# A transformer block with self- and cross-attention: where the context norm is turned, which output goes first, and when weights and x are asked for

## The chip, the cores and the metric

The kernel runs on one core of a Trainium2 chip. The metric is the device time in microseconds (us) of one execution. A core has a matrix engine (PE, or TensorE), a vector engine (DVE), a scalar engine (ACT), a general engine (POOL, or GpSimd) and a queue engine (SP) which issues nearly all DMA transfers here. Each engine works through its own list of instructions in the order in which the program wrote them; an instruction that waits holds up everything behind it on the same engine.

## The reference

All is float32, with B = 2 batches, S = 1024 positions, width D = 256, a context of T = 154 positions of width 192, 16 heads of 64, and a feed-forward width of 1024.

```python
h = layernorm(x, ln1_g, ln1_b)
x = attention(h, h, sa_wq, sa_wk, sa_wv, sa_wo, sa_bo) + x
h = layernorm(x, ln2_g, ln2_b)
x = attention(h, ctx, ca_wq, ca_wk, ca_wv, ca_wo, ca_bo) + x
h = layernorm(x, ln3_g, ln3_b)
p = h @ ff_w1 + ff_b1
a, gate = p[..., :1024], p[..., 1024:]
out = (a * gelu(gate)) @ ff_w2 + ff_b2 + x
# attention: q, k, v by heads; softmax(q k^T / 8) v; heads joined; @ wo + bo
```

## The kernel before

The work is written out by hand in program order; no scheduler moves it. It has three loops, and the pieces of other stages are laid between their steps.

**Self-attention** goes over 16 units (two batches times eight pairs of heads), each in 8 slots, so there are 128 attention slots, numbered p from 0. A slot treats 128 queries of a pair of heads, in two groups of 64. It begins with `self_first`: 32 score matmuls (L465) into two PSUM tiles `s`, and two maxima on DVE (`st`, L627). Then `then()` writes four exponentials on ACT (L476, with their sums). Since a row of scores is split over two groups of partitions, the maxima and sums have to be swapped between them: `exchange` (L486), four small DMAs on SP, issued when the slot's exponentials are done. One slot later `join` corrects for the two maxima (POOL `dd`, ACT `ee`, POOL `zz` and `den`), DVE takes a reciprocal (`rd`, L573) and POOL scales the exponentials (L577). Two slots later DVE transposes them into `pT` (L591), and `self_values` multiplies by v (`po`, L512). The reciprocal is written on DVE ahead of the next slot's maxima, and `ee` on ACT behind the next slot's exponentials, so an exchange that lands late holds up both engines.

The slots of the first half of a unit (n = 0, 1, and in unit 0 up to 3) and those at n = 4, 5 have no `self_values`; there `run_work` puts in the next unit's projections (`pq_sa`, `pk_sa`, L348, `pv_sa`, L379), a step of a norm from the list `side`, and output projections (`py`, L443) from the list `outs`. v's projection of units 1 to 3 is made in two halves, each in a slot of its own. When v is complete, two DMAs of 256 KB in all exchange its halves between partitions (L392, L393).

After `then()` a slot takes one entry of the list `later` (in every slot below 32, afterwards in three slots of eight), and then `load_ahead` asks for the weights of the unit after next: q at slot n = 2 of a unit, k at 3, v at 7 (q and k three slots later in unit 0). All of these are issued on SP behind the slot's exchange. `load_ahead_parts` (L146) makes the loads of the second batch's x (eight tiles of 128 KB) and of sa_wo (eight chunks of 128 KB), which `later` holds from the start, after unit 1's k and q weights and an empty entry.

**Cross-attention** goes over the same 16 units in three slots each, n = 0, 1, 2: 48 cross slots, numbered c. A slot makes scores of up to three tiles against 154 context positions (`sc`, L746), maxima (`neg`), up to six exponentials on ACT (L762), and a slot later their scaling on POOL (L773); DVE transposes them (L789), SP regroups them (L806), and `cross_weigh` at n = 1 multiplies by v (`cross_values`, `poc`, L825). What lies beside:

- n = 0: q of the next unit (`pq_ca`, copied to SBUF by ACT at the next slot, L363);
- n = 1: k of the next unit (`pk_ca`, L690), a step of `side`, the context's v in every other unit (`pv_ca`, L706, copied by three ACT instructions, L715 and L716), up to two outputs, then `poc`;
- n = 2: a step of `side`, and up to two outputs.

A step of a norm (`norm_pieces`, `norm_beside`) takes the statistics of two tiles on DVE, the deviation on POOL, normalises two tiles (`xn`, on POOL for the second batch's context norm at L253, on ACT for the feed-forward norm at L256), and turns two earlier ones: four transposes on PE into one PSUM bank (`ph`, L266), which ACT copies into `hT` with gain and shift (L281). The copies of a step (`store`) wait in the list `stores`, which is flushed after the next slot's scores, or at n = 1 ahead of `poc`, behind the slot's exponentials. A step that turns needs a PSUM bank: `run_work(n, n_side, bank, n_sum)` gives it `bank`, or spends one of its n `mm` banks; without either it stops at such a step and takes no step behind it.

PSUM has three rings of two: `s` (two banks each), `mm` and `po` (one bank each; `mm_tile` and `sum_tile`). A ring gives its buffers in turn, so a matmul that opens a buffer waits until the one before has been copied out. From the third unit on, `pk_ca` uses `po`'s ring, as do the first half of `poc` (two banks), the steps that turn, and the outputs counted by n_sum. The second half of `poc` uses `mm`.

**The feed-forward part** runs in 64 slots (`pa`, L907; `pf`, L930). At the seam between self- and cross-attention, the first cross slot begins with `cross_keys` of unit 1, which needs that unit's ca_wk; the tile for k weights has one buffer, that for q weights two.

Of the kernel before, what the change touches and what calls it, by code (L numbers as in the profile page):

```python
# [18 lines left out]
def tile_transformer_block(ctx: ExitStack, tc: tile.TileContext, a: dict, out: bass.AP):  # L19
    nc = tc.nc  # L20
# [8 lines left out]
    NPAIR = DA // (2 * DH)  # L29
# [13 lines left out]
    QG = 2 * KB  # L43
# [101 lines left out]

    def load_ahead_parts():  # L146

        wo["sa"] = const.tile([P, NPAIR, D], F32, tag="wo", name="sa_wo")

        def tile_of_x(t):  # L150
            nc.sync.dma_start(
                out=xt[B - 1, t // GT][:, t % GT, :], in_=x[B - 1, t * P:(t + 1) * P, :])

        def chunk(i):
            nc.sync.dma_start(out=wo["sa"][:, i, :], in_=w["sa_wo"][i * P:(i + 1) * P, :])

        return ([lambda t=t: tile_of_x(t) for t in tile_order("sa")],
                [lambda i=i: chunk(i) for i in range(NPAIR)])

    for what in "qkv":  # L160
        load_weights("sa", 0, what)
# [128 lines left out]
    def tile_order(kind):  # L290

        if kind == "ff":
            return list(range(NT))
        return [t for i in range(NT // 2) for t in (i, NT // 2 + i)]
# [75 lines left out]
            else:  # L370
                nc.scalar.copy(dk, own)  # L371

    def project_self_values(v, pv, wt, h, i0, n):

        for i in range(i0, i0 + n):
            for c in range(NH):
                for r in range(2):
                    own = slice(r * HR, (r + 1) * HR)
                    nc.tensor.matmul(  # L379
                        pv[r][:, i * P:(i + 1) * P], lhsT=h[own, c, i * P:(i + 1) * P],  # L380
                        rhs=wt[own, c, :], start=(c == 0), stop=(c == NH - 1),
                        tile_position=(r * HR, 0),
                    )

        def store():
            tiles = [slice(r * GT + i0, r * GT + i0 + n) for r in range(2)]
            for r in range(2):
                nc.scalar.copy(
                    v[:, tiles[r], 0, :],
                    pv[r][:, i0 * P:(i0 + n) * P].rearrange("p (t d) -> p t d", d=P))  # L390
            if i0 + n == GT:
                nc.sync.dma_start(out=v[:QG, :, 1, :], in_=v[QG:, :, 0, :])  # L392
                nc.sync.dma_start(out=v[QG:, :, 1, :], in_=v[:QG, :, 0, :])  # L393

        return store

# [29 lines left out]

        return [costing(2, q), costing(2, k)] + value_pieces(b, pr, parts)

    def value_pieces(b, pr, parts):
        n = GT // parts  # L430
        return [
            costing(2, lambda i=i: project_self_values(
                qk["sa", b, pr][2], two_banks(f"pv_sa{b}_{pr}_{i}"), wsl["sa", pr, "v"],
                hT["sa", b], i * n, n))
            for i in range(parts)
        ]

# [223 lines left out]
    def load_ahead(p):  # L661

        ui, n = divmod(p, 2 * SH)
        for what in "qkv":
            at = {"q": 2, "k": 3, "v": 2 * SH - 1}[what] + 3 * (ui == 0 and what != "v")
            if n != at:
                continue
            if ui + 2 < NU:
                load_weights("sa", units[ui + 2][1], what)
            elif ui + 2 == NU or what == "q":  # L670
                load_weights("ca", units[ui + 2 - NU][1], what)
        if p >= SA - 2:
            load_weights("ca", units[1][1] if p == SA - 2 else units[2][1], "kq"[p - SA + 2])


    CG = [(t, min(TG, NT - t)) for t in range(0, NT, TG)]
# [275 lines left out]
    with tc.manual_schedule():  # L952
# [46 lines left out]
        take("k", 0)  # L999
        part("k", 3)  # L1000
        take("k", 2)
        tiles, chunks = load_ahead_parts()
        later.append(lambda: load_weights("sa", units[1][1], "k"))
        later.append(lambda: load_weights("sa", units[1][1], "q"))
        later.extend([lambda: None] + tiles + chunks)
        side.append((True, (), turn_rows))
        side.extend((True, (), lambda b=b: turn_context(b)) for b in range(B))
        work.append(costing(2, lambda: self_queries(*units[0], P, 2 * P)))
        work.extend(value_pieces(*units[0], 2))

        for p in range(SA):
            if p % (2 * SH) == 0:
                self_beside(p // (2 * SH))
            if p == SA - SH:
                work.extend(held)
                held.clear()
            then = self_first(p)
            flush(stores)
            late = then()
            if p >= LAG:  # L1020
                turn_groups(p - LAG)
            flush(adds)
            if late:
                late()
            if later and (p < 2 * SH * HP or p % (2 * SH) in (2, 4, 6)):
                later.pop(0)()
            load_ahead(p)
            h, hg = divmod(p, SH)
            if h == 0 or hg < LAG:

                run_work(2 if p < SA - SH else 1, h % 2 or h == 0, sum_tile)
                if p == LAG:
                    load_weights("sa", units[1][1], "v")
            else:
                run(lambda: self_values(h - 1, hg - LAG))

        for c in range(CA):
            if c == 0:
                pTc["ring"] = pt_.tile(
                    [P, 2 * NK, QH // 2], F32, tag="pT", name="pT_ca"  # L1040
                ).rearrange("p a b -> p (a b)")[:, :3 * 2 * NB * NT * KB].rearrange(
                    "p (u n j q) -> p u n j q", u=3, n=NB, j=2)
            if c == SH + 1:
                out_pieces("sa", B - 1, 1, tile_order("ca"))
                outs.append(lambda: load_out("ca"))
            if c == SH + 1:

                w1, w2, parts = hold_gated()
                add_biases("ca", 0)
                others = later[:] + [lambda: None] * (len(parts) - len(later))  # L1050
                later[:] = [fn for pair in zip(parts, others) for fn in pair] + others[len(parts):]
            ui, n = divmod(c, len(CG))
            nxt = units[ui + 1] if ui + 1 < NU else None
            if n == 0:
                cross_beside(ui)
            elif n == 1 and 1 <= ui < NU - 2:
                load_weights("ca", units[ui + 2][1], "q")
            elif n == 2:
                for i, what in ((2, "k"), (1, "v")):
                    if 1 < ui + i < NU:  # L1060
                        load_weights("ca", units[ui + i][1], what)
            if c == 0:
                run(lambda: cross_keys(*nxt))
            flush(adds)
            then = cross_first(c)
            flush(stores)
            if c == 1:
                turn_groups(SA - 2)
            if n == 1 and ui > 1 and nxt:
                run(lambda: cross_keys(*nxt, sum_tile))  # L1070
                flush(stores)
            flush(drain)
            flush(lates)
            lates.append(then())
            if c == 0:
                drain.append(scale_groups(*joins.pop(0)))
            if c == 2:
                turn_groups(SA - 1)
            cross_drain(c)
            if c == 1:  # L1080
                run(lambda: cross_queries(*nxt))
            elif c == 2:
                run(lambda: cross_queries(*units[2], bank=sum_tile))
            elif c == 3:
                run(lambda: self_values(2 * NU - 1, 0))
            elif c == 4:
                run(lambda: self_values(2 * NU - 1, 1))
                run(lambda: cross_keys(*nxt, sum_tile))
            elif n == 0 and ui:
                if nxt:  # L1090
                    run(lambda: cross_queries(*nxt))
                run_work(0, 1)
            elif n == 1:

                run_work(0, 1, sum_tile)
                if ui % 2 == 0:
                    run(lambda: context_values(*units[ui]))
                run_work(0, 0, n_sum=1)
                run_work(1, 0)
                flush(adds)  # L1100
                flush(stores)
                cross_weigh(c)
            elif n == 2:
                run_work(0, 1, sum_tile)
                if len(outs) > 2:
                    run_work(2, 0)
            cross_regroup(c)
            for _ in range(min(2, len(later))):
                later.pop(0)()
# [58 lines left out]
```

## Time and profile before

| what | us |
|---|---|
| median of 3 runs (1149.77 to 1154.18) | 1152.45 |
| profiled execution | 1153.73 |
| its span, first to last instruction | 1151.9 |

The stretches of the profiled span, by where the first score matmul of a unit or stage starts, and how much of each PE is busy:

| stretch | length | PE busy | DVE busy | ACT busy |
|---|---|---|---|---|
| start, to the first scores | 17.55 | 13.17 | 9.05 | 7.59 |
| unit 0 | 44.64 | 40.90 | 33.05 | 28.49 |
| unit 1 | 46.69 | 43.82 | 39.49 | 27.71 |
| unit 2 | 43.28 | 40.91 | 39.22 | 28.39 |
| unit 3 | 43.83 | 41.40 | 39.75 | 30.01 |
| units 4 to 15 | 524.73 | 522.21 | 474.72 | 347.24 |
| cross-attention, from the seam | 231.64 | 218.93 | 147.56 | 136.16 |
| feed-forward | 199.54 | 195.02 | 53.42 | 41.03 |

A line of a list of waits names the engine, its tile and line, who ended the wait, and then the total in us, the number of times and the longest. A line of a timeline has its start, its length, the engine, line and operation, the tiles as out<-in, shapes and a count; in brackets stands the idle time ahead of it and who ended it. A line of windows has the stretch, its length, and then for PE, weight loads, DVE, ACT and POOL the busy us with the number of instructions, then the granted clock of PE, the share of the DMA engines that is busy, and GB/s.

### The profile page before, as it was taken

The page shows a single profiled execution, that of the slowest core. Times are in us where ns is not written, and L with a number is a line of the kernel's source. Part 1 is how long each engine was busy: PE and PEld are TensorE (multiplying, and loading weights), DVE is VectorE, ACT ScalarE, POOL GpSimd, SP SyncE. Part 2 cuts the span into 40 slices and gives each one's busy share as a digit, 9 for nine tenths or more (in the row PEclk, how much of TensorE's full clock was granted, in tenths as well). Part 3 has the DMA queues.
Part 4 walks back from the last instruction along what each step waited for, and adds up shares of the span by engine and source line. Part 5 has one row for each costly group of instructions (what it writes and reads, how often), then busy time and mean ns, then how long its engine had stood idle before and what let it go on. Part 6 is the DMA issues. An engine that isn't in the chain of part 4 may idle for free.

```text
span 1151.9 us, 36754 instructions
## 1 busy us (share of the span) xinstructions
PE 1116.4 (97%) x14372; PEld 687.6 (60%) x14372; DVE 836.3 (73%) x1183; ACT 646.6 (56%) x2082; POOL 675.9 (59%) x1568
## 2 busy tenths in 40 slices
PE   8899999999999999999999999998999989999998
PEld 6444444545545545545445554675667667888887
DVE  4888998898888998999898889665666764232222
ACT  5665666666765665666666666557555571041111
POOL 2666777778777877777777777656454443020000
PEclk9999999999999999999999999999999999999999
DMA  3222112101111111111111110257554533000000
GB/s 88 62 68 67 35 31 47 41 13 40 39 23 40 33 28 45 31 30 40 31 30 40 25 28 15 65 141 188 137 119 115 119 78 74 10 10 10 19 10 19
DMA packets 104910, 59.94 MB, mean 52 GB/s; under 512 B 32090, under 2 KB 95522, under 8 KB 104738
## 3 DMA queue, kind: packets, MB, share of 16 engines
q1 hardware_dynamic: 103506, 56.93, 20.8%
q8 instruction: 114, 1.87, 0.7%
q10 hardware_dynamic: 1232, 0.66, 0.2%
q14 instruction: 58, 0.48, 0.1%
HBM read 27.91 MB, written 2.10 MB: 26 GB/s over the span
## 4 chain that ended last, share of the span: by engine, by line
PE 80%; ACT 7%; DVE 4%; DMA 3%; issue 2%; POOL 2%; SPq 2%; DVEq 0%; ACTq 0%; POOLq 0%
PE po L512 17%; PE s L465 17%; PE pa L907 10%; PE py_sa L443 5%; PE pf L930 5%; PE py_ca L443 4%; PE pk_sa L348 4%; PE pq_sa L348 4%; PE poc L825 4%; PE pv_sa L379 4%; ACT p L476 3%; PE pq_ca L348 3%; ACT p L762 2%; PE sc L746 2%; DMA st<-st 2%
## 5 line engine op out<-in xcount | busy, mean ns | idle before, releaser
L476 ACT ACTIVATE p<-s,st 128x512 f32<-128x512 f32 x512 | 345.2, 686 | 205.1 <-DVE st L627 201.5
L577 POOL TENSOR_SCALAR p<-p,rd,ee 128x512 f32<-128x512 f32 x512 | 387.5, 774 | 45.1 <-DVE rd L573 44.0
L627 DVE TENSOR_REDUCE st<-s 128x2 f32<-128x1024 f32 x256 | 301.2, 1218 | 36.0 <-PE s L465 24.9
L591 DVE STREAM_TRANSPOSE pT<-p 128x1024 f32<-128x1024 f32 x256 | 302.2, 1218 | 0.4 <-POOL p L577 0.3
L465 PE MATMUL s<-k_sa,q_sa 64*32 64x512 f32 x4096 | 253.2, 596 | 12.7 <-ACT p L476 11.9
L512 PE MATMUL po<-pT,v_sa 64*64 64x256 f32 x4096 | 236.7, 380 | 0.0
L512 PEld LDWEIGHTS po<-pT,v_sa 64*64 64x64 f32 x4096 | 150.7, 133 | 109.9 <-issue 31.0
L773 POOL TENSOR_SCALAR p<-p,rden 128x154 f32<-128x154 f32 x256 | 97.4, 404 | 101.2 <-DVE rden L770 100.7
L762 ACT ACTIVATE p<-sc,neg 128x154 f32<-128x154 f32 x256 | 96.9, 418 | 91.3 <-DVE rden L770 84.9
L465 PEld LDWEIGHTS s<-k_sa,q_sa 64*32 64x32 f32 x4096 | 65.4, 106 | 136.5 <-issue 66.0
L907 PE MATMUL pa<-hT_ln,wf 128*128 128x256 f32 x512 | 120.7, 379 | 0.0
L916 DVE SCALAR_TENSOR_TENSOR u<-pa,cols,gate 128x256 f32<-128x256 f32 x64 | 30.9, 483 | 123.2 <-ACT gate L913 123.2
L913 ACT ACTIVATE gate<-pa,cols 128x256 f32<-128x256 f32 x64 | 30.3, 474 | 148.8 <-PE pa L907 148.8
L907 PEld LDWEIGHTS pa<-hT_ln,wf 128*128 128x128 f32 x512 | 96.9, 190 | 13.1 <-issue 0.2
L476 ACT ACTIVATION_READ_ACCUMULATOR p<-s,st 128x1 f32 x512 | 103.8, 203 | 0.0
L379 PEld LDWEIGHTS pv_sa<-sa_wv,hT_ln 64*128 64x128 f32 x1024 | 59.7, 188 | 18.7 <-DMA st<-st 9.2
L500 POOL TENSOR_TENSOR zz<-ee,st 128x8 f32<-128x8 f32 x128 | 26.0, 203 | 70.4 <-ACT ee L498 70.4
L930 PE MATMUL pf<-wf,u 128*128 128x256 f32 x256 | 65.2, 379 | 0.2 <-DVE u L916 0.2
L379 PE MATMUL pv_sa<-sa_wv,hT_ln 64*128 64x128 f32 x1024 | 63.7, 276 | 1.5 <-ACT k_sa L371 1.3
L751 DVE TENSOR_REDUCE neg<-sc 128x6 f32<-128x924 f32 (+1 forms) x48 | 48.0, 1003 | 17.6 <-PE sc L746 17.6
L762 ACT ACTIVATION_READ_ACCUMULATOR p<-sc,neg 128x1 f32 x256 | 59.8, 233 | 0.0
L443 PE MATMUL py_ca<-ca_wo,o_ca 128*128 128x256 f32 x256 | 58.3, 381 | 1.3 <-DVE o_ca L838 1.0
(87 smaller groups left out, 1259.7 us busy)
## 6 DMA issues: line engine op xcount, KB each, us to landing
wf<-pT_ca SPq DMA_DIRECT2D x128, 128.0 KB, 2.4
st<-st SPq DMA_DIRECT2D x512, 1.0 KB, 1.8
v_sa<-v_sa SPq DMA_DIRECT2D x32, 256.0 KB, 3.4
sa_wq<-in_L_xattn_sa_wq_dram SPq DMA_DIRECT2D x32, 128.0 KB, 2.9
sa_wk<-in_L_xattn_sa_wk_dram SPq DMA_DIRECT2D x32, 128.0 KB, 2.9
sa_wv<-in_L_xattn_sa_wv_dram SPq DMA_DIRECT2D x32, 128.0 KB, 2.9
ca_wq<-in_L_xattn_ca_wq_dram SPq DMA_DIRECT2D x32, 128.0 KB, 2.9
wf<-in_L_xattn_ff_w_dram SPq DMA_DIRECT2D x12, 256.0 KB, 3.7
```

The source lines that it names most:

```text
L348: nc.tensor.matmul(pq[r][f:f + m, at:at + n], lhsT=wt[own, c, f:f + m], rhs=h[own, c, t0:t0 + n], start=(c == 0), stop=(c == NH - 1), tile ...
L379: nc.tensor.matmul(pv[r][:, i * P:(i + 1) * P], lhsT=h[own, c, i * P:(i + 1) * P], rhs=wt[own, c, :], start=(c == 0), stop=(c == NH - 1), ...
L443: nc.tensor.matmul(py[:, :D], lhsT=o[:, i, t * P:(t + 1) * P], rhs=wo[kind][:, half * HP + i, :], start=(i == 0), stop=(i == HP - 1),)
L465: nc.tensor.matmul(sc[a4 * KB:(a4 + 1) * KB, j, :], lhsT=q[r, c:c + KB], rhs=k[r, h * HB:(h + 1) * HB], start=True, stop=True, tile_positi ...
L476: nc.scalar.activation(pr[:, j, :], sc[:, j, :], AF.Exp, bias=st[:, 0, 0, i, j:j + 1], accum_out=st[:, 0, 1, i, j:j + 1],)
L512: nc.tensor.matmul(po[a2][j * DH:(j + 1) * DH, :QH // 2], lhsT=v[r, t, e, j * DH:(j + 1) * DH], rhs=pT[r, j * NK + n, :], start=(t == 0 an ...
L577: nc.gpsimd.tensor_scalar(pr[:, j, :], pr[:, j, :], rd[:, c:c + 1], ee[:, 0, c:c + 1], op0=ALU.mult, op1=ALU.mult,)
L591: nc.vector.transpose(halves[h][:, :, c:c + KB], groups.pop(0).rearrange("p j (n k) -> p (j n) k", k=KB))
L627: nc.vector.tensor_reduce(st[:, 0, 0, i, :], sc[i], AX.X, ALU.max, negate=True)
L762: nc.scalar.activation(pr_[:, j, i, :T], sc[:, j, i * T:(i + 1) * T], AF.Exp, bias=neg[:, j, i:i + 1], accum_out=den[:, j, i:i + 1],)
L907: nc.tensor.matmul(pa[:, half, :TF * P], lhsT=w1[:, c, half * DF + f * P:half * DF + (f + 1) * P], rhs=h[:, c, t0 * P:(t0 + TF) * P], star ...
L930: nc.tensor.matmul(sums[blk][i][:, :D], lhsT=sums[blk, "u"][:, f, i * P:(i + 1) * P], rhs=w2[:, f, :], start=(f == 0), stop=(f == NF - 1),)
```

## The change

Four things change; no arithmetic does.

- The loads of the second batch's x and of sa_wo leave the list `later`. `load_ahead_parts` gives them as a table by slot: slots n = 0, 1, 4, 5 of units 1 to 4, x first (8, 9, 12, 13, 16, 17, 20, 21), then sa_wo (24, 25, 28, 29, 32, 33, 36, 37). Unit 1's k and q weights are in the same table at slots 0 and 1.
- The move of v's halves in unit 0 is not issued where v is stored, but put into `later`, from which the same slot takes it behind its exchange.
- At the seam, the k weights of cross unit 1 and the q weights of unit 2 are asked for in slots 125 and 126 in place of 126 and 127.
- In the cross slots a step that turns may run at n = 0, in a bank of `po`'s ring, and no longer at n = 1. At n = 1 the output in `po`'s ring goes ahead of the context's v in place of behind it.

```diff
-        return ([lambda t=t: tile_of_x(t) for t in tile_order("sa")],
-                [lambda i=i: chunk(i) for i in range(NPAIR)])
+        pieces = ([lambda t=t: tile_of_x(t) for t in tile_order("sa")]
+                  + [lambda i=i: chunk(i) for i in range(NPAIR)])
+        slots = [u * 2 * SH + n for u in range(1, HP + 1) for n in (0, 1, 4, 5)]
+        return dict(zip(slots, pieces))
...
-    def project_self_values(v, pv, wt, h, i0, n):
+    def project_self_values(v, pv, wt, h, i0, n, soon):
...
             if i0 + n == GT:
-                nc.sync.dma_start(out=v[:QG, :, 1, :], in_=v[QG:, :, 0, :])
-                nc.sync.dma_start(out=v[QG:, :, 1, :], in_=v[:QG, :, 0, :])
+                move()
+
+        def other_half():
+            nc.sync.dma_start(out=v[:QG, :, 1, :], in_=v[QG:, :, 0, :])
+            nc.sync.dma_start(out=v[QG:, :, 1, :], in_=v[:QG, :, 0, :])
+
+        def move():
+            if soon:
+                other_half()
+            else:
+                later.append(other_half)
...
-        if p >= SA - 2:
-            load_weights("ca", units[1][1] if p == SA - 2 else units[2][1], "kq"[p - SA + 2])
+        if p in (SA - 3, SA - 2):
+            load_weights("ca", units[p - SA + 4][1], "kq"[p - SA + 3])
...
-        tiles, chunks = load_ahead_parts()
-        later.append(lambda: load_weights("sa", units[1][1], "k"))
-        later.append(lambda: load_weights("sa", units[1][1], "q"))
-        later.extend([lambda: None] + tiles + chunks)
+        ahead = load_ahead_parts()
+        ahead[0] = lambda: load_weights("sa", units[1][1], "k")
+        ahead[1] = lambda: load_weights("sa", units[1][1], "q")
...
-        work.extend(value_pieces(*units[0], 2))
+        work.extend(value_pieces(*units[0], 2, False))
...
             if later and (p < 2 * SH * HP or p % (2 * SH) in (2, 4, 6)):
                 later.pop(0)()
+            if p in ahead:
+                ahead[p]()
             load_ahead(p)
...
             elif n == 0 and ui:
                 if nxt:
                     run(lambda: cross_queries(*nxt))
-                run_work(0, 1)
+                run_work(0, 1, sum_tile)
             elif n == 1:
 
-                run_work(0, 1, sum_tile)
+                run_work(0, 1, n_sum=1)
                 if ui % 2 == 0:
                     run(lambda: context_values(*units[ui]))
-                run_work(0, 0, n_sum=1)
                 run_work(1, 0)
```

More of the change, by code (lines that the diff above doesn't have):

```diff
@@ L427, in self_pieces, with value_pieces @@
         return [costing(2, q), costing(2, k)] + value_pieces(b, pr, parts)
-    def value_pieces(b, pr, parts):
+    def value_pieces(b, pr, parts, soon=True):
         n = GT // parts
@@ L433, in value_pieces @@
                 qk["sa", b, pr][2], two_banks(f"pv_sa{b}_{pr}_{i}"), wsl["sa", pr, "v"],
-                hT["sa", b], i * n, n))
+                hT["sa", b], i * n, n, soon))
             for i in range(parts)
```

## The prediction

> **What bounds the kernel now.** I read the page's busy shares, then the engines' waits, then TensorE's timeline around each gap, then windows of the granted clock.
>
> ```profile
> PE 1116.4 (97%) x14372; PEld 687.6 (60%) x14372; DVE 836.3 (73%) x1183; ACT 646.6 (56%) x2082; POOL 675.9 (59%) x1568
> POOL dd L494 <- DMA st<-st: 45.9, 48, 13.7
> PE poc L825 <- ACT hT_ln L281: 5.8, 3, 3.0
> PE pv_ca L706 <- ACT q_ca L363: 2.9, 6, 1.2
> PE pk_ca L690 <- DMA ca_wk<-in_L_xattn_ca_wk_dram: 2.3, 1, 2.3
> ...
> 45.50 0.20 POOL L494 TENSOR_TENSOR dd<-st 128x4 f32<-128x4 f32 x1 [2.37 <-DMA st<-st]
> 46.96 4.32 PE L379 MATMUL pv_sa<-sa_wv,hT_ln 64*128 64x128 f32 x64 [1.34 <-ACT k_sa L371]
> 63.05 0.20 POOL L494 TENSOR_TENSOR dd<-st 128x4 f32<-128x4 f32 x1 [2.22 <-DMA st<-st]
> 95.77 1.09 PE L465 MATMUL s<-k_sa,q_sa 64*32 64x512 f32 x16 [1.52 <-ACT p L476]
> 98.85 4.61 PE L512 MATMUL po<-pT,v_sa 64*64 64x256 f32 x64
> 142.08 3.68 PE L512 MATMUL po<-pT,v_sa 64*64 64x256 f32 x64
> ...
> 789.88 1.22 PE L825 MATMUL poc<-wf,v_ca 64*64 64x256 f32 x10 [1.73 <-ACT hT_ln L281]
> 806.11 0.86 PE L825 MATMUL poc<-wf,v_ca 64*64 64x256 f32 x10 [2.99 <-ACT hT_ln L281]
> 930.14 1.99 PE L706 MATMUL pv_ca<-ca_wv,ctxT 96*128 96x256 f32 x8 [1.23 <-ACT q_ca L363]
> 948.90 0.86 PE L825 MATMUL poc<-wf,v_ca 64*64 64x256 f32 x10 [1.07 <-ACT hT_ln L281]
> ...
> 789.00:791.00 2.00, 1.12 (x16) 0.75 (x20) 0.00 (x0) 1.75 (x6) 1.85 (x6) 0.82 0.76 249
> 791.00:793.00 2.00, 2.00 (x24) 1.22 (x20) 0.85 (x2) 0.00 (x0) 0.34 (x1) 0.50 0.41 99
> ```
>
> TensorE is busy 97%, so only its gaps (35 us in all) and its slow stretches can be won. The second group shows the statistics exchange landing late in units 0 and 1, and the same 64 matmuls taking 4.61 us after a gap and 3.68 otherwise. The third shows TensorE waiting for the norm's copies (hT_ln) and for q_ca; the last, a clock (the eighth figure) of 0.50 just after such a wait.
>
> [...]after the gaps at 789 and 806, clocks of 0.82/0.50/0.83 and 0.58/0.56 over 2 us windows lose 1.7 us each. [...]1.52 us at 95.77 was enough, in unit 3 the same gap (183.55) was not. [...]Slot 6's exchange agrees: issued at 58.98 after two moves of v, it let POOL go only at 63.05. [...]
>
> **Part 1: x and output weights in spread slots, v's move one place later.** Same DMAs, other order on SP; unit 1's k and q weights stay in slots 0 and 1, so nothing changes before slot 3. Before, attention slots 3 to 10 each carry an x tile and 11 to 18 a chunk of wo, beside weights in 2, 5, 6, 7, 10, 11, 15; after, they sit at 0, 1, 4, 5 of units 1 to 4, never with a weight load. Unit 0: v's move (38.21 to 39.5) stands ahead of slot 3's exchange, whose issue takes 4.11 us instead of about 2.5; POOL is late by 2.37, the exponential of the maxima (ACT) waits, k_sa's copy behind it, and PE idles 1.34. With the move behind, the exchange lands near 43, before ACT is free (44.1): gain 1.3. Unit 1 lasts 46.69 us (62.19 to 108.88), unit 2 43.28, with the same number of scores: 3.4 more. It holds four late exchanges (2.22, 1.03, 1.00, 0.98) and a half clock (4.61 less 3.68, and 1.81 for 16 scores against 1.09: 1.65). x loads leave slots 3 to 7 and 10, so most of these go, but x enters 12 and 13. Units 2 and 3 get loads that they lacked; unit 1 had wo chunks in its slots 12 to 15, and there POOL waited 0.33 or less after the first; I charge 0.5. Their own gaps of 1.12 and 1.52 stay: VectorE is busy 39.2 of 43.3 us there. Sum 1.3 + 3.4 - 0.5 = 4.2; I take 3.5, as some lateness of unit 1 is VectorE's own. Ends: 1 and 5. x is read four or more slots after its load, wo's first half at slot 37 after loads in 24 to 29.
>
> **Part 2: seam weights a slot sooner.** ca_wk of unit 1 is issued at 719.87, behind slot 126's exchange and v_ca's two moves; PE waits 2.29 until 723.01, with VectorE idle 3.04 and ACT behind. A slot earlier SP is at about 713, and the buffer's last reader finished before 704. The wait goes. What is late next is slot 127's exchange (issued 721.50, landed 725.28): it has q's two loads (1.39) ahead now instead of k's (1.46), and its exponential stands behind six of the first cross slot, ending near 725.9. Gain 2.1; ends 1.3 and 2.3.
>
> **Part 3: cross slots.** At n = 1 no turning step runs any more; at n = 0 one may, on a sum bank. By the queue's rules the second batch's context norm turned in cross slots 11, 13, 14, 16 and now in 11, 12, 14, 15; the first feed-forward norm in 41, 43, 44, 46 and now 41, 42, 44, 45. The four transposes (0.6 us) and their copies are the same; only order changes. Taken one by one:
> - Slot 12/13: PE finishes pq at 783.10 and waits for xn, ready on POOL at 783.75: 0.65 new. ACT runs q's copies to 785.87, then hT to 787.3, k to 787.6. PE does sc, pk, pv to 787.8 and starts poc without the 1.73. No output is waiting here, so poc's second half needs pv's bank, copied after six exponentials at 791.0: 1.6 new. The slot ends near 792.6 against 794.31: +1.7, or 0 if the clock halves.
> - Slot 15/16: pq ends 799.94, transposes and sc, pk to 802.1; ACT finishes q at 802.0, hT 803.5, k 803.7. PE idles 1.5 where it idled 3.4. End 806.85 against 810.27: +3.4, or +1.7 with a half clock.
> - pv's 0.33 in four plain units (slots 19, 25, 31, 37) lies behind the output now ahead of it (1.8 us of PE): +1.3.
> - Slot 42/43 is the place where the change costs. The bank ring has two: pk takes the one of slot 41's turn, the output that of slot 42's. ACT after six exponentials (929.46) does xn 1.0, q's copies 0.96, hT 0.9: free at 932.35, with the six exponentials of slot 43 behind. PE has done pk at 928.9 and waits 3.4 for the output's bank; pv and poc queue behind it. End of the output block 937.8 against 935.52: -2.3, with a probable half clock -4.0.
> - Slot 45/46: the turn waits for xn to 942.46 (before: sc waited 1.01), then outputs cover ACT's hT, and poc's 1.07 goes: end 950.15 against 951.64, +1.5.
>
> Sum with one of the first two at half clock: 1.7 + 3.4 - 1.7 + 1.3 - 4.0 + 1.5 = 2.2. Ends: -3 (all three at half clock, and slot 16 waiting as before) and +7 (none). VectorE, POOL and the regroup DMAs keep their work; POOL's scales of slot 12 shift by 2 us, hidden: VectorE turns them only in slot 14.
>
> **Sum.** 3.5 + 2.1 + 2.2 = 7.8 us. The profiled execution took 1153.73 (span 1151.9, 1.8 around it), so 1145.9; against the runs' median of 1152.45, 1.3 lower, 1144.6. I say 1144.5.
>
> **Rivals.**
> - *The new bank wait eats the cross gain, and part 1 gives little.* For it: ACT is busy without a break in 783 to 791 and 797 to 806, so the norm's copies only change place; VectorE is near its limit in units 1 to 3. Against: ACT sits idle in 791 to 796, so it is order and not load. Cross -1, part 1 1.5, seam 2.1: 2.6 less, about 1149.8.
> - *Everything lands.* No new half clock, units 0 and 1 like unit 2: 5 + 2.3 + 6 = 13, about 1139. Against: three gaps of 1.5 us or more remain.
> - *Slower: the order is kept by whole buffer, not by region.* Then slots 12, 13, 20, 21 each load a slice of the x buffer whose other slice VectorE normalises in that slot, and stats would wait for the exchange and the load, about 5 us each on an engine with 10% slack, and the outputs at slot 37 for a chunk issued after slot 37's exchange: PE is there at 225.6, exponentials end near 229, exchange 2.5, landing 2.3, so 8 us and 1.7 of half clock. 20 + 10 - 8: about 1175. It decides from the first such slot. Against it: poc reads wf while feed-forward weights land in other slices of wf, and neither waits for the other in the list of waits.
>
> **How the numbers follow.** Forecast 0.58 (own range 1140 to 1149), bank wait 0.24, everything lands 0.10, whole buffer 0.05, and 0.03 for bank waits dear enough to end above before. A measurement here can tell about 0.5% (5.8 us) from no change, so faster means below 1146.7. The forecast is there in three cases of four (0.44), the bank rival one in four (0.06), the third always (0.10): 0.60 with little more from the spread of runs, so 0.62. Slower takes 0.05 and 0.03 and some of the bank rival's upper end, 0.09; the same 0.29. The range 1138.5 to 1151.5 leaves out the whole-buffer case, both cases' tails and the extreme good one.
>
> **What would show it.** Right: no wait of pk_ca for ca_wk; dd waits in units 0 and 1 under 0.5 us and unit 1 near 44 us; poc waiting for hT 1.6 us at most; a py_ca wait of 3 us for hT at slot 43. Wrong: stats in slot 12 or py in slot 37 waiting for a DMA; a wait at slot 13 for pv's bank above 3 us; unit 1 still at 46.

## The result, and the profile after

The changed kernel took 1144.66 us in the median of six runs (1140.85 to 1146.27), the kernel before 1152.22 beside it (1149.77 to 1154.9): ratio 0.9929, with a 95% interval of 0.9908 to 0.995. That is 7.6 us. The two profiled executions, 1153.73 and 1144.58 us, are 9.1 apart (spans 1151.9 and 1142.8).

The page's busy times and then the list of waits, the rows that answer to those of before (after the colon: total us, how many, longest us):

```profile
PE 1112.5 (97%) x14372; PEld 688.5 (60%) x14372; DVE 835.4 (73%) x1183; ACT 647.0 (57%) x2082; POOL 672.7 (59%) x1568
```

```profile
POOL dd L508 <- DMA st<-st: 46.9, 47, 14.1
...
PE py_ca L457 <- ACT hT_ln L286: 3.2, 1, 3.2
PE ph_ln L271 <- POOL xn_ln L258: 2.1, 3, 0.9
...
PE ph_ln L271 <- ACT xn_ln L261: 1.7, 2, 1.5
PE poc L839 <- ACT hT_ln L286: 1.3, 1, 1.3
PE poc L839 <- ACT v_ca L730: 1.0, 1, 1.0
...
PE po L526 <- DVE pT L605: 0.8, 1, 0.8
```

The counts of instructions are the same. Three rows of before are gone: k's weights at the seam, pv_ca behind q_ca, and two of the three waits of poc for hT_ln. In their place stand new ones, all smaller but for the 3.2 us of py_ca: besides it the rows of ph_ln, v_ca's copy, and po behind pT. The row of dd says little (46.9 against 45.9): it adds up POOL's waits wherever they stand, and not what TensorE loses by them. It takes POOL's and TensorE's timelines to see what changed in units 0 and 1:

```profile
44.04 0.20 POOL L508 TENSOR_TENSOR dd<-st 128x4 f32<-128x4 f32 x1 [0.57 <-DMA st<-st]
60.78 0.20 POOL L508 TENSOR_TENSOR dd<-st 128x4 f32<-128x4 f32 x1 [1.41 <-DMA st<-st]
105.67 0.20 POOL L508 TENSOR_TENSOR dd<-st 128x4 f32<-128x4 f32 x1 [2.07 <-DMA st<-st]
```

```profile
45.92 3.90 PE L384 MATMUL pv_sa<-sa_wv,hT_ln 64*128 64x128 f32 x64
...
92.80 1.09 PE L479 MATMUL s<-k_sa,q_sa 64*32 64x512 f32 x16 [1.52 <-ACT p L490]
94.13 1.96 PE L479 MATMUL s<-k_sa,q_sa 64*32 64x512 f32 x16 [0.24 <-ACT p L490]
96.02 4.45 PE L526 MATMUL po<-pT,v_sa 64*64 64x256 f32 x64
100.40 1.95 PE L479 MATMUL s<-k_sa,q_sa 64*32 64x512 f32 x32
102.28 3.68 PE L526 MATMUL po<-pT,v_sa 64*64 64x256 f32 x64
```

Slot 3's exchange is late by 0.57 us where it was 2.37, and TensorE's 1.34 us behind it, at pv_sa, is gone. Unit 1's first exchange is late by 1.41 instead of 2.22. A new late one, 2.07 us, stands at the end of unit 1. And in this profile, as in the one before, there is a half clock in unit 1: 16 scores in 1.96 us where 1.09 is usual, and 64 value matmuls in 4.45 where 3.68 is, at a granted clock of 0.83 over 90 to 100 us (before: 0.83 over 97 to 107).

The seam and the cross slots that the prediction goes through, in TensorE's timeline:

```profile
718.07 0.79 PE L704 MATMUL pk_ca<-ctxT,ca_wk 96*128 96x154 f32 x4
729.59 3.68 PE L526 MATMUL po<-pT,v_sa 64*64 64x256 f32 x64 [0.79 <-DVE pT L605]
...
779.63 0.66 PE L271 MATMUL ph_ln<-ident,xn_ln 128*128 128x128 f32 x4 [0.56 <-POOL xn_ln L258]
786.63 0.86 PE L839 MATMUL poc<-wf,v_ca 64*64 64x256 f32 x10 [1.04 <-ACT v_ca L730]
797.44 1.26 PE L839 MATMUL poc<-wf,v_ca 64*64 64x256 f32 x16 [1.27 <-ACT hT_ln L286]
...
834.47 1.89 PE L457 MATMUL py_ca<-ca_wo,o_ca 128*128 128x256 f32 x8
836.20 1.89 PE L720 MATMUL pv_ca<-ca_wv,ctxT 96*128 96x256 f32 x8
837.93 1.89 PE L457 MATMUL py_ca<-ca_wo,o_ca 128*128 128x256 f32 x8
...
920.68 3.44 PE L457 MATMUL py_ca<-ca_wo,o_ca 128*128 128x256 f32 x8 [3.23 <-ACT hT_ln L286]
923.97 1.89 PE L720 MATMUL pv_ca<-ca_wv,ctxT 96*128 96x256 f32 x8
934.13 0.33 PE L271 MATMUL ph_ln<-ident,xn_ln 128*128 128x128 f32 x1 [1.50 <-ACT xn_ln L261]
```

pk_ca at the seam waits for nothing, but a value block 11.5 us later now waits 0.79 us for the transposed p. Slots 12 and 13 have waits of 0.56 and 1.04, slot 16 has 1.27 where slots 13 and 16 had 1.73 and 2.99. The middle group is a plain slot: pv stands between the two halves of the output and waits for nothing. At slot 43 the output waits 3.23 us, the dearest single wait of the new order. ACT's timeline shows why, and the windows (sixth figure after the stretch and its length: granted clock) show what follows:

```profile
917.64 1.11 ACT L261 ACTIVATE xn_ln<-x,off_ln,rstd_ln 128x256 f32<-128x256 f32 x2
918.62 1.10 ACT L368 ACTIVATE q_ca<-pq_ca 128x512 f32<-128x512 f32 x2
919.58 1.05 ACT L286 ACTIVATE hT_ln<-ph_ln,cols 128x256 f32<-128x256 f32 x2
920.47 0.34 ACT L708 COPY k_ca<-pk_ca 128x154 f32<-128x154 f32 x1
```

```profile
918.00:920.00 2.00, 0.00 (x0) 0.00 (x0) 1.27 (x3) 2.00 (x5) 1.90 (x6) 1.00 0.00 0
920.00:922.00 2.00, 1.32 (x3) 1.14 (x4) 0.00 (x0) 2.00 (x10) 0.44 (x2) 0.56 0.00 0
922.00:924.00 2.00, 2.00 (x7) 1.59 (x7) 0.00 (x0) 1.04 (x6) 0.00 (x0) 0.58 0.00 0
924.00:926.00 2.00, 2.00 (x11) 1.76 (x10) 0.42 (x1) 0.11 (x1) 0.00 (x0) 1.00 0.00 0
```

TensorE does nothing in 918 to 920 while ACT runs the norm's normalisation, q's copies and the norm's copies in a row; the output starts only when the last of these has emptied its bank, and the next 4 us run at a clock of 0.56 and 0.58: the output's eight matmuls take 3.44 us, 1.89 elsewhere. What stands behind the waiting output on TensorE is held up with it: pv_ca, next in the program, starts only at 923.97, 4.25 us after q's copies ended at 919.72, and where pv stands ahead of the output it is q's copies that it waits for (1.21 us in the mixed order below).

Comparing where the same instructions start in both profiles, self-attention up to the seam is 2.65 us shorter, the seam up to the fourth cross slot 1.55, and the cross slots 4.95. Together 9.15, which is the difference of the two profiled executions.

### The profile page after: what moved, and what is told of

It is laid out like the page before. It is cut to its first block, busy times and chain, and to the rows that moved or that the text cites. A ratio compares the mean times of both kernels' runs of the same rounds, so it can differ in the third digit from the quotient of the medians.

```text
span 1142.8 us, 36749 instructions
## 1 busy us (share of the span) xinstructions
PE 1112.5 (97%) x14372; PEld 688.5 (60%) x14372; DVE 835.4 (73%) x1183; ACT 647.0 (57%) x2082; POOL 672.7 (59%) x1568
## 4 chain that ended last, share of the span: by engine, by line
PE 85%; ACT 5%; DVE 3%; DMA 2%; POOL 2%; SPq 1%; issue 1%; DVEq 0%; POOLq 0%; ACTq 0%
PE po L526 18%; PE s L479 18%; PE pa L921 10%; PE py_sa L457 5%; PE py_ca L457 5%; PE pf L944 5%; PE pk_sa L353 4%; PE pq_sa L353 4%; PE pv_sa L384 4%; PE poc L839 4%; PE pq_ca L353 3%; ACT p L490 2%; PE sc L760 2%; SPq L500 1%; DVE st L641 1%
## 5 line engine op out<-in xcount | busy, mean ns | idle before, releaser
L457 PE MATMUL py_ca<-ca_wo,o_ca 128*128 128x256 f32 x256 | 60.7, 388 | 4.3 <-ACT hT_ln L286 3.2
L457 PE MATMUL py_sa<-sa_wo,o_sa 128*128 128x256 f32 x256 | 59.5, 385 | 0.0
```

The source lines that it names most:

```text
L457: nc.tensor.matmul(py[:, :D], lhsT=o[:, i, t * P:(t + 1) * P], rhs=wo[kind][:, half * HP + i, :], start=(i == 0), stop=(i == HP - 1),)
```

## The experiments

My theory before the runs: the three parts act apart from each other, each through the waits named, and what is left over is the half clock. Its rivals: part 1 does nothing that lasts, and the whole comes from the seam and the cross slots; or the cross order gains nothing, because its new bank waits give all back. All runs are compared with the kernel before, run beside them.

### Each part alone

Part 1 alone (the loads in slots 0, 1, 4, 5 of units 1 to 4, and v's move behind the exchange):

```diff
+        slots = [u * 2 * SH + n for u in range(1, HP + 1) for n in (0, 1, 4, 5)]
+        return dict(zip(slots, pieces))
...
+                later.append(other_half)
...
+            if p in ahead:
+                ahead[p]()
```

> Part 1 alone: x and output weights in spread slots and v's move of unit 0 behind the exchange; seam and cross slots as before. Theory (parts are independent and add up): the self-attention stretch ends about 2.5 us sooner, and nothing changes after it, so 2.5 to 3.5 us faster than before, about 1149.5. Rival (most of the whole change's gain is here, by fewer half clocks): 5 us or more. Rival (part 1 only moves the lateness to unit 2): under 1 us.

Part 2 alone:

```diff
-        if p >= SA - 2:
-            load_weights("ca", units[1][1] if p == SA - 2 else units[2][1], "kq"[p - SA + 2])
+        if p in (SA - 3, SA - 2):
+            load_weights("ca", units[p - SA + 4][1], "kq"[p - SA + 3])
```

> Part 2 alone: the seam's weights one slot sooner. Theory: pk_ca no longer waits 2.3 us for ca_wk, and a new wait of under 1 us of po for pT follows three slots later, so 1.5 us faster, about 1150.7. Rival (the seam's wait is hidden anyway, DVE sets the pace there): no gain at the end of cross slot 3.

Part 3 alone:

```diff
-                run_work(0, 1)
+                run_work(0, 1, sum_tile)
...
-                run_work(0, 1, sum_tile)
+                run_work(0, 1, n_sum=1)
...
-                run_work(0, 0, n_sum=1)
```

> Part 3 alone: transposes at n = 0, output ahead of the context's v. Theory: 5 us faster, about 1147.3, made of +2 at slots 12 to 14, +3.7 at 15 to 17, +1.8 by pv behind an output, -3.8 at slot 43, +1.2 at 46. Rival (the cross gain depends on the earlier parts' shift of phase): under 2 us. Rival (the loss at slot 43 comes by chance of the clock): slot 43 loses 2.3 only.

Measured: part 1 1151.55 (0.9974, 0.9963 to 0.9986), part 2 1150.72 (0.9973, 0.9963 to 0.9983), part 3 1151.74 (0.9973, 0.9962 to 0.9985). By these ratios each is worth about 3 us of 1154.07, and the three together 9.2, where the whole change has 0.0071 of 1154, 8.2; by the medians they are 2.5, 3.4 and 2.3, together 8.2, where the whole has 7.6. No interval of the three reaches 1, so all three parts carry, both rivals fall, and no large interaction between the parts is needed.

Part 2's timeline has both of the seam's effects, so the new wait of the value block comes with this part and needs no loads of part 1:

```profile
718.76 0.79 PE L690 MATMUL pk_ca<-ctxT,ca_wk 96*128 96x154 f32 x4
729.91 3.69 PE L512 MATMUL po<-pT,v_sa 64*64 64x256 f32 x64 [0.42 <-DVE pT L591]
```

Part 3's waits in its slots are those of the whole change to 0.05 us (0.56, 1.08, 1.32, 3.27, 1.51 against 0.56, 1.04, 1.27, 3.23, 1.50). Yet in this profile, of 1151.98 us, the cross slots up to 41 are 6.5 us shorter than before and slots 42 to 47 lose 5.7 of it. The windows have the cause:

```profile
920.00:930.00 10.00, 6.74 (x29) 5.34 (x29) 3.10 (x8) 7.43 (x31) 3.85 (x12) 0.70 0.01 2
930.00:940.00 10.00, 8.49 (x87) 6.16 (x85) 5.09 (x12) 3.38 (x13) 2.18 (x6) 0.96 0.42 92
```

After the wait of 3.27 us the mean clock is 0.70 over 10 us: in steps of 2 us it is at 0.50 from about 924 to 931, two half-clock stretches on end, where the whole change's profile has one (920 to 924 above). A third falls behind the 1.51 us at 940. The waits repeat with the order; the half clock behind them does not (0.70 here over 920 to 930, 0.83 in the whole change's profile).

### Part 1 taken apart

v's move alone, behind slot 3's exchange, with x and the output weights where they were:

```diff
+                after_exchange.append(other_half)
...
+            flush(after_exchange)
```

> Only v's move of unit 0 behind the exchange of slot 3; x and output weights in slots 3 to 18 as before. Theory: PE's wait of 1.34 us in unit 0 goes, unit 1's late exchanges stay: 1.3 us faster at the end of unit 0, about 1151. Rival (the x loads, not v's move, made slot 3's exchange late): the wait of 1.34 stays and nothing is gained.

The spread slots alone, with v's move where it was:

```diff
-        work.extend(value_pieces(*units[0], 2, False))
+        work.extend(value_pieces(*units[0], 2))
```

> Part 1 without v's move: x and sa_wo in spread slots, unit 0's v moved at once as before; seam and cross as before. Theory: PE's wait of 1.3 us in unit 0 stays, units 1 to 3 are about 1 us shorter: 1 to 1.5 us faster than before. Rival (the loads' place is the whole of part 1): 3 us faster, and unit 0's wait gone.

Measured: the move alone 1153.56 (0.9992, 0.9982 to 1.0002), the slots alone 1153.79 (0.9997, 0.9988 to 1.0006); neither can be told from no change, and together they gave 0.9974. The timelines of TensorE show the move doing what it should. The slots alone keep unit 0's wait:

```profile
46.95 4.32 PE L384 MATMUL pv_sa<-sa_wv,hT_ln 64*128 64x128 f32 x64 [1.25 <-ACT k_sa L376]
```

With the move alone that wait is gone, but late exchanges stay or come up in the slots that follow, in POOL's timeline:

```profile
50.53 0.20 POOL L503 TENSOR_TENSOR dd<-st 128x4 f32<-128x4 f32 x1 [1.62 <-DMA st<-st]
61.84 0.20 POOL L503 TENSOR_TENSOR dd<-st 128x4 f32<-128x4 f32 x1 [1.44 <-DMA st<-st]
```

The move now stands in a slot that also carries an x tile: the DMA queue of SP shows the two moves at 41.83 and 42.96, an x tile at 43.64, and the next exchange only at 44.81. In this profile 1.3 us are won in unit 0 and 2.3 in unit 1, and 1.8 of them are lost again in unit 2. But unit 1 has no half clock here, which was worth 1.65 in the profile before; without that next to nothing is left at the end of unit 2. That the loss comes from the x tile is not shown. Whether the two pieces need each other or merely add up is not settled: 0.9 and 0.3 make 1.2 of 3.0 us, but corrected for the clock (below) it is 0.8 and 1.1 of 2.8.

### Part 3 taken apart

The whole change, but the output behind context values again:

```diff
-                run_work(0, 1, n_sum=1)
+                run_work(0, 1)
                 if ui % 2 == 0:
                     run(lambda: context_values(*units[ui]))
+                run_work(0, 0, n_sum=1)
                 run_work(1, 0)
```

> The changed kernel, with the output at n = 1 behind the context's v again (turning at n = 0 kept). Theory (pv's 0.33 us waits in slots 19, 25, 31, 37 come back, and in slot 43 pv fills part of the 3.2 us that the output waits for hT): 1.3 us lost in the plain units, 1.3 won at slot 43, so equal to the changed kernel, about 1144.7, or 1.7 faster if slot 43 keeps the full clock. Rival (the output ahead is what saves slot 43): slower than the changed kernel by 2 us or more.

The whole change, but the turning step at n = 1 again:

```diff
-                run_work(0, 1, sum_tile)
+                run_work(0, 1)
...
-                run_work(0, 1, n_sum=1)
+                run_work(0, 1, sum_tile, n_sum=1)
```

> The changed kernel, with the turning steps at n = 1 again (output ahead of context's v kept). Theory: poc's waits for hT at slots 13 and 16 come back with 1.7 and 3 us and a half clock or two, 5.7 us lost there; slot 43 wins back 3 of its 3.8: 2 to 3 us slower than the changed kernel, about 1147.5. Rival (turning at n = 0 brings nothing on balance because of slot 43): equal to the changed kernel or faster.

Measured: output behind 1148.04 (0.9947, 0.9931 to 0.9963), turn back 1149.24 (0.9957, 0.9943 to 0.9971). Both medians lie above those of the whole change (1144.66, and 1146.51 when it was run again), though the intervals overlap; at equal clock (table below) both are some 3 us dearer. So both edits of part 3 earn something. With the output behind, the plain slots have the old 0.33 us back in TensorE's timeline, and pv is longer by 0.1:

```profile
836.49 1.99 PE L720 MATMUL pv_ca<-ca_wv,ctxT 96*128 96x256 f32 x8 [0.33 <-ACT q_ca L368]
838.32 3.62 PE L457 MATMUL py_ca<-ca_wo,o_ca 128*128 128x256 f32 x16
```

Each such slot became 0.59 us longer, not 0.33: the recorded idle time was not the whole price of these stops. Slots 42 to 44, where pv now waits 1.85 us for q, won 1.15 back, so that the cross slots of the two profiles are only 0.75 us apart; the other 1.4 of their 2.2 us stand ahead of slot 12. This variant was expected to come out equal, and why it is some 3 us dearer is shown only in part. With the turn back, slot 16 has its old wait, slots 12 to 18, up to k's projection in 19, lose 6.1 us against the whole change, and slots 42 to 47 win 2.0 of it back: the output's bank at slot 43 is now the one that k's copy empties, which stands on ACT behind q's copies alone:

```profile
802.16 1.55 PE L839 MATMUL poc<-wf,v_ca 64*64 64x256 f32 x10 [2.99 <-ACT hT_ln L286]
...
925.42 1.99 PE L457 MATMUL py_ca<-ca_wo,o_ca 128*128 128x256 f32 x8 [1.89 <-ACT k_ca L708]
```

So the change gains with the context norm (slots 11 to 16) and pays with the feed-forward norm (41 to 46), as predicted.

### Slot 43

Three ways to shorten the 3.23 us. The norm's copies ahead of q's:

```diff
                 run_work(0, 1, sum_tile)
+                stores.reverse()
```

> The changed kernel, with ACT copying a turned norm (hT) ahead of the next unit's q where a step turned at n = 0. Theory (the waits at slots 16 and 43 are ACT's order, q's 1.0 us ahead of hT): slot 43's wait falls from 3.2 to 2.2 us and slot 16's from 1.3 to 0.3; pv in slot 13 waits 1 us more but that lies behind v's copies; 2 us faster than the changed kernel, 3.7 if slot 43 keeps the full clock: 1141 to 1143. Rival (the waits only move to pv and q): equal.

The first output on the other bank where a turn was made:

```diff
-                run_work(0, 1, n_sum=1)
+                swap = turned["at"] == ui
+                run_work(0, 1, n_sum=0 if swap else 1)
+                if swap:
+                    run_work(1, 0)
...
-                run_work(1, 0)
+                run_work(0 if swap else 1, 0, n_sum=1 if swap else 0)
```

> The changed kernel, where a step turned at n = 0 the first output takes an mm bank and the one in the sum ring goes behind the context's v. Theory (only the bank that the turn holds makes slot 43 wait): the wait falls from 3.2 to about 1.9 us, for q's first copy, and the clock stays full: 1.3 to 3 us faster than the changed kernel, about 1142.5. Rival (the mm bank waits as long): equal, slot 43 still at half clock.

The same in the feed-forward norm's slots only, with q's copies ahead of the norm there:

```diff
+                if ui > HP + 1 and side and side[0][0]:
+                    flush(stores)
```

> The changed kernel; at slot 42 q's copies on ACT go ahead of the norm's step, and slot 43's first output takes an mm bank. Theory (slot 43 waits for ACT's order): the wait falls from 3.2 to about 1.1 us and the clock stays full there: 2.5 to 3.7 us faster than the changed kernel, about 1141.5. Rival (the wait moves to the second output's bank): under 1 us.

Measured: 1146.1 (0.9925, 0.9909 to 0.9941), 1144.35 (0.992, 0.9904 to 0.9936) and 1142.12 (0.99, 0.9886 to 0.9915). The first output at slot 43, one line from each kernel's timeline of TensorE, in this order:

```profile
919.79 3.24 PE L457 MATMUL py_ca<-ca_wo,o_ca 128*128 128x256 f32 x8 [2.27 <-ACT hT_ln L286]
```

```profile
919.54 3.14 PE L457 MATMUL py_ca<-ca_wo,o_ca 128*128 128x256 f32 x8 [1.85 <-ACT q_ca L368]
```

```profile
917.08 1.99 PE L457 MATMUL py_ca<-ca_wo,o_ca 128*128 128x256 f32 x8 [0.86 <-ACT q_ca L368]
```

The wait shrinks to 2.27, 1.85 and 0.86 us, so it is the bank's release by ACT and the order of ACT's copies that set it. Only in the last is the output itself at full clock (1.99 us for its eight matmuls; 3.24 and 3.14 in the others). The first two have no clear gain over the changed kernel; the third is 4.4 us below it in its own series (1146.51, below). One thing that eats the gain shows in the last two: there poc's matmuls come in groups of 2 to 14 instead of 16 and 8, and the block takes 3.3 us instead of 2.75. With the bank swapped, VectorE adds the late second output at 926.72 to 927.14, while poc starts at 926.61. That poc's later bank waits for this is the author's reading; TensorE's timeline records no wait there.

Then the order of before in the feed-forward norm's slots alone, where it was the better one, and the change everywhere else:

```diff
-                run_work(0, 1, sum_tile)
+                run_work(0, 1, None if ui > HP + 1 else sum_tile)
...
-                run_work(0, 1, n_sum=1)
+                old = bool(ui > HP + 1 and side and side[0][0])
+                if old:
+                    run_work(0, 1, sum_tile)
+                else:
+                    run_work(0, 1, n_sum=1)
...
+                if old:
+                    run_work(0, 0, n_sum=1)
```

> The changed kernel, but the feed-forward norm (slots 41 to 46, where outputs are pending) is turned as in the kernel before, with the output behind pv in those slots alone. Theory (the change costs 2.65 us there and wins all else): slot 43 waits 1.2 us for q and keeps its full clock; 2.65 us faster than the changed kernel, about 1142. Rival (the loss at slot 43 is hidden by what follows): equal.

And, in the same series, the changed kernel as it is:

> The changed kernel once more, beside the next three on one chip. Theory: 0.993 of before; self-attention about 2.5 us shorter than before, cross 5 us shorter, with a half clock at slot 43 (1.7 us) in this run too, and others in self-attention by chance.

Measured: 1140.89 (1140.59 to 1141.77; 0.989, 0.9877 to 0.9904), and the changed kernel 1146.51 (0.9937, 0.9924 to 0.9949). The mixed order is 5.6 us faster than the change in the same series, and the fastest of all. TensorE's timeline and windows of the mixed order at the same place:

```profile
917.42 1.99 PE L720 MATMUL pv_ca<-ca_wv,ctxT 96*128 96x256 f32 x8 [1.21 <-ACT q_ca L368]
919.25 3.62 PE L457 MATMUL py_ca<-ca_wo,o_ca 128*128 128x256 f32 x16
...
936.16 0.86 PE L839 MATMUL poc<-wf,v_ca 64*64 64x256 f32 x10 [1.05 <-ACT hT_ln L286]
```

```profile
920.00:930.00 10.00, 8.99 (x99) 6.64 (x98) 5.95 (x14) 5.79 (x20) 3.17 (x9) 1.00 0.39 86
```

It waits 1.21 us instead of 3.23 and stays at full clock. Between the two orders slots 42 to 47 differ by 2.7 us in these profiles, half clock included, so that alone can't make 5.6 us. Each run lists its mean granted clock:

| kernel | runs | mean us | mean clock | us at full clock, estimated |
|---|---|---|---|---|
| before, all series of the experiments | 78 | 1153.96 | 0.9954 | 1150.4 |
| part 1 / part 2 / part 3 alone | 11 / 16 / 22 | 1151.5 / 1151.1 / 1151.1 | 0.9949 / 0.9958 / 0.9949 | 1147.6 / 1147.8 / 1147.2 |
| v's move alone / slots alone | 14 / 13 | 1153.5 / 1153.5 | 0.9949 / 0.9946 | 1149.6 / 1149.3 |
| output behind / turn back | 6 / 6 | 1147.8 / 1149.2 | 0.9963 / 0.9945 | 1145.0 / 1145.0 |
| changed kernel, first / again | 6 / 5 | 1144.3 / 1146.4 | 0.9963 / 0.9944 | 1141.4 / 1142.1 |
| norm's copies first / bank swapped | 6 / 6 | 1145.5 / 1144.8 | 0.9955 / 0.9973 | 1142.0 / 1142.8 |
| q early and swap | 5 | 1142.2 | 0.9984 | 1141.0 |
| mixed order | 4 | 1141.0 | 0.9998 | 1140.9 |

The last column is an estimate: within the kernels a run's time falls by 0.77 us for each 0.001 of clock (one line through all 198 runs, each about the mean of its own kernel), and the column takes each mean to a clock of 1. The standard errors of this column are 0.1 to 0.4 us, 0.7 for the swapped bank. For the changed kernel this takes the six runs' standard deviation from 1.9 to 0.5 us, so most of its spread is half clock. Its one run at a clock of 1.000 took 1140.85 us, which is the mixed order's time. At equal clock the three parts are worth 2.8, 2.6 and 3.2, together 8.6, against 8.3 to 9.0 for the whole. The two edits of part 3 are another matter: with only one of them the kernel stands at 1145.0, just where parts 1 and 2 alone would put it (1150.4 less 2.8 and 2.6). By this estimate neither earns anything without the other; the profiles don't show why.

## Why the prediction was right, and where its terms were off

It said 1144.5, and 1144.66 came out. The mechanisms it named are in the traces, but the terms were off in both directions and cancelled, so that it came so near is luck.

- **Part 1: 3.5 predicted, 2.65 in the profiles, 2.8 alone at equal clock.** Unit 0 gave 1.47 (1.3 predicted): unit lengths 44.64 and 43.17. Unit 1 gave 1.53, from 46.69 to 45.16, where 3.4 was counted. That term was mis-sized: it held 1.65 us of half clock as an effect of the late exchanges, and the half clock is in unit 1 after the change too, behind the unchanged 1.52 us wait at 92.80. The late exchanges became shorter instead of going away, and 2.07 us at 105.67 is new; so "dd waits under 0.5 us" was wrong. In units 2 to 15 this pair of profiles has unit 2 losing 0.77, unit 3 winning 0.23, the rest 0.2, against a charge of 0.5.
  The other profiles show how much of this is chance. Nine have the new order of self-attention (the changed kernel twice, part 1 alone, and the six variants built on the changed kernel), three the old one (before, and parts 2 and 3 alone). From q's projection in one unit to that in the next, unit 1 takes 42.5 to 43.7 us in eight of the nine, and 45.15 only in the profile above, the one with a half clock there; in the old order it takes 46.69, 43.58 and 44.72. So "unit 1 near 44" did come true, but the 3.4 us was read from a profile whose unit 1 was dear by chance, and the 0.77 lost in unit 2 is no cost of the new order, which takes 44.05 to 44.70 there, the other two old profiles 44.65 and 44.71. Unit 0's gain of 1.3 stands where no half clock falls in it (44.49 twice, against 43.04 to 43.52). Units 0 to 2 together are 2.2 us shorter in the mean of the nine than in that of the three.
- **Part 2: 2.1 predicted, 1.55 in the profiles, 2.6 alone at equal clock.** The wait of 2.29 went entirely. What was late next is what the prediction named, slot 127's exchange: POOL waits for it, then ACT's exponential of the maxima for POOL, then VectorE's reciprocal, and at the end of that chain stands the transposed p for which TensorE waits 0.79.

```profile
723.43 0.20 POOL L508 TENSOR_TENSOR dd<-st 128x4 f32<-128x4 f32 x1 [0.63 <-DMA st<-st]
724.16 0.21 ACT L512 ACTIVATE ee<-dd 128x8 f32<-128x8 f32 x1 [0.78 <-POOL dd L510]
724.96 0.18 DVE L587 RECIPROCAL rd<-den 128x4 f32<-128x4 f32 x1 [0.64 <-POOL den L516]
```

The step that was mis-sized is the issue of q's two loads ahead of that exchange: taken at 1.39 us, it took SP 2.24 here (717.24 to 719.48). In the nine profiles with the new seam (part 2 alone, the changed kernel twice and its six variants) TensorE doesn't wait in two (the changed kernel again, the mixed order), waits 0.27 to 0.60 us in six, and 0.79 in this one. So 1.55 comes from the worst of nine, and the changed kernel run again wins the whole wait. Why part 2 alone came to 2.6 at equal clock, more than the wait itself (1.40 to 2.29 us in the profiles that ask as before), stays open.

- **Part 3: 2.2 predicted, 4.95 in the profiles, 3.2 alone at equal clock, within the stated ends.** The waits came out as worked out: 0.56 for 0.65, 1.04 for 1.6, 1.27 for 1.5, 3.23 for 3.4, 1.50 for 2. Slots 12 to 14 gave 2.05 (1.7), slots 15 to 17 gave 3.68 (3.4), the plain slots 0.59 each, 1.77 for three of them, with 0.1 from another (1.3 predicted for four), slots 42 to 44 lost 3.8 (4.0), slots 45 to 47 gave 1.15 (1.5). These make 4.95, 2.75 more than predicted: 1.7 that was set aside for a half clock at slot 13 or 16, which did not fall in this profile, 0.57 for the stops' real price, and the rest small errors of the slots. With the same two banks in the ring the wait at slot 43 fell from 3.23 to 2.27 us by the order of ACT's copies alone.
- **The rivals.** The bank wait is there, but eats 3.8 of some 8.7 and not all. "Everything lands" (1139) missed in part because the clock did not stay full: the run at a clock of 1.000 came within 2 us of it, and the rest is not clock. Tracking by whole buffer is refuted for these places: no statistics wait for an x tile of the second batch (the only wait of st_ln for x is 4.2 us, for the first tile of all), and py waits for no chunk of wo (py_sa starts at 223.2 us while chunks are issued until 229.2, and none of its idle time ends on a DMA).

The prediction called a half clock after slot 43's wait probable. In the profiles it follows each of the three waits of 3.2 us (the whole change twice, part 3 alone), once or twice over; but one timed run of the changed kernel had a clock of 1.000, where a single half-clock stretch would have left 0.9985 (an estimate: 1.7 us of 1143). So, if that run had the wait as both profiles do, it doesn't follow always.

What stays open: whether v's move and the spread slots need each other, and whether the mixed order's clock of 0.9998 comes from slot 43 alone. At equal clock it is only 0.6 to 1.2 us ahead of the changed kernel; the rest of its lead is clock. Three of its four runs had a clock of 1.000, and the profiled one a single half-clock stretch, in unit 0 behind a wait of 1.59 us. Its cross slots hold no wait above 1.27 us, and in all profiles no wait below 1.3 us was followed by a half clock (last section); for the timed runs this is argued, not shown.

## What to carry to other kernels

One order for all steps of a kind was not the best here: the same move won 5.7 us where no output stood behind it in the ring of banks and lost 3.8 where one did (the half clocks of these profiles included: two of before in the first, one of the changed kernel in the second), and choosing by place beat both kernels. Before pricing a gap, ask whether the slow stretch behind it would be there anyway; price a half clock as a chance per gap (in these profiles it followed 0 of 66 waits of 0.8 to 1.3 us, 11 of 55 up to 1.65 and 19 of 24 above), and compare kernels by time and mean clock together. A wait that is taken away can uncover the next one, so look some slots further and follow it back to its first cause: here the 0.79 us recorded against VectorE was a DMA issue some 0.8 us longer than expected, several engines earlier. And take a unit's length from several profiles before explaining it: identical self-attention reached the seam between 716.95 and 719.79 us.

## What was unexpected of the hardware

- A stop of TensorE recorded as 0.33 us idle cost 0.59 in each plain slot. From the start of k's projection to the start of the matmuls behind it 1.12 us pass where it is 0.63 without the stop: 0.49, of which the record calls only 0.33 idle, because without the stop the recorded times of the two overlap by 0.16 (in the changed kernel pk_ca ends at 834.63 and py_ca starts at 834.47). The other 0.10 is in pv's own eight matmuls (1.99 us instead of 1.89).
- A half clock did not follow every wait, and it followed the longer ones more often. After slot 45's wait of 1.50 us, the same in both profiles of the changed kernel, it fell in one (0.83 over 930 to 940) and not in the other (1.00). In the 14 profiles, between the first scores and 960 us, these waits of TensorE of 0.8 us and more were followed by one (it began at the latest 4 us after the wait, or within it):

| wait, us | waits | followed by half clock |
|---|---|---|
| 0.8 to 1.3 | 66 | 0 |
| 1.3 to 1.65 | 55 | 11 |
| 1.65 to 2.0 | 11 | 8 |
| 2.0 to 2.3 | 4 | 2 |
| 2.98 to 3.27 | 9 | 9 |

- A half-clock stretch takes 1.7 us of clock (0.83 over 10 us), which is 0.0015 of a run's mean; by the line through all runs, 0.77 us for 0.001, that costs a run about 1.1 us (an estimate). The two profiles of the changed kernel have two stretches each, the one of before three, the one of part 3 alone five.
- Two stretches can follow one wait: in part 3 alone, 3.27 us of wait came with some 6.8 us at a clock of 0.50. So it was in five of the nine waits of about 3 us, and in all five the clock had halved more than 1 us before the wait was over; in the other four it halved between 0.4 us before the wait's end (the changed kernel) and 1.2 us after it (before), and one stretch followed.
